# LayerNorm's transposed tiles copied whole by ScalarE and scaled in SBUF by GpSimd, four shared PSUM banks for TensorE's products, and one convolution chunk on TensorE in 5 bands of 15 instead of 7

## The chip, the cores and the metric

The kernel runs on one core of one Trainium2 chip. The metric is device time in microseconds (us); lower is better. The core has five engines with an instruction queue each, executed in order: TensorE (PE in the profile; PEld is its weight load), VectorE (DVE), ScalarE (ACT), GpSimd (POOL) and SyncE (SP, which here only issues DMAs). Engines wait for one another by semaphores. TensorE's results land in PSUM, of which this kernel uses eight banks; VectorE and ScalarE read PSUM and SBUF, GpSimd reads SBUF alone in this kernel.

## What is computed

One transformer block on images, float32, for `x` of shape (16, 128, 96, 96): 16 images, 128 channels, 96 by 96 pixels.

```python
def _ffn(xn_nchw, w_in, w_dw, w_out):
    h1 = jnp.einsum('bchw,oc->bohw', xn_nchw, w_in[:, :, 0, 0])           # 128 -> 512 channels
    h2 = lax.conv_general_dilated(h1, w_dw, ..., feature_group_count=HID) # 3x3, each channel by itself
    h3 = jax.nn.gelu(h2, approximate=False)
    return jnp.einsum('bchw,oc->bohw', h3, w_out[:, :, 0, 0])             # 512 -> 128
...
xn1 = _layernorm(x_hwc, ln1_w, ln1_b)              # over the 128 channels of a pixel
attn_out = _attention(xn1, wq, wk, wv, wp)         # channel attention: 8 heads of 16 x 16
x = x + attn_out.transpose(0, 3, 1, 2)
xn2 = _layernorm(x_hwc, ln2_w, ln2_b).transpose(0, 3, 1, 2)
x = x + _ffn(xn2, w_in, w_dw, w_out)
```

`_layernorm` subtracts the mean over the channels and divides by the square root of the variance plus 1e-5.

## The kernel before

**Tiling.** Channels lie on the 128 partitions, pixels along the free dimension. An image has 8 bands of 12 rows (1152 pixels); 16 images give 128 bands. A band has three units of 4 rows (384 pixels) and 9 blocks of 128 pixels. A quad is four such blocks (`QT = 4`, 512 pixels); an image has 18 quads, and each goes through LayerNorm twice (`norm`, with `second` false and true; the profile's names end in `_a` and `_b`), so there are 576 quads in all.

**LayerNorm of one quad** (functions `pixels` and `channels` inside `norm`). `forth` (L642) has TensorE transpose the four 128 x 128 blocks into one PSUM bank `tr`, pixels then on the partitions. `stats` (L649) has VectorE take mean and variance, two blocks per `bn_stats` instruction, directly out of that bank. GpSimd adds the epsilon (`variance`, L656), takes the power -0.5 (`power`, L660) and, in the second norm, computes minus the mean (L664) and the shift (L668). `scaled` (L700, L704) has ScalarE read each block from the bank and write it, scaled, to an SBUF tile `zT`: four instructions of 128 x 128. Only then is the bank free for the next quad. For the first norm `gram` (L714) multiplies the scaled blocks with themselves for the attention. `back` (L753) transposes three blocks (a unit) back into a bank `h`, and `place` (L757, L759) has ScalarE copy them to the padded image tile `xn`. For image 0 the transposes go to the accumulator's banks, and VectorE scales two of the four blocks (`also_scaled`, L687 and L691).

**Attention and second sum.** `attention` is a short chain of small steps per image. `x2` then multiplies a unit of `xn` with the image's 128 x 128 matrix (`mix`, L595); ScalarE writes the result (`mixed`, L604), and a GpSimd-issued DMA adds `x` to it in place (`add_x`, L607).

**Feed-forward.** The 512 hidden channels are four chunks of 128. A chunk of a band is one job (`conv_job`): three matmuls for the hidden values (`hidden`, L940) into banks `h`, ScalarE copies them to a padded tile (`kept`, L945; `halo`, L936), and the nine taps of the 3 x 3 filter are shared out. ScalarE multiplies three taps (`products`, L956). GpSimd adds one of them to the centre tap (`merge`, L959), and issues two accumulating DMAs that add the others to one another and to the result (L978, L981). VectorE runs five taps: the first from SBUF with the merged tile into the PSUM accumulator `acc` (L965), three that add into `acc` (L969), and the last from `acc` to the SBUF tile `h3` (L965 too). ScalarE applies gelu (L985). In the first chunk of every eighth band, 16 jobs in all, GpSimd and not ScalarE multiplies the third tap (`POOL_THIRDS`, L954).

In some bands, chosen by `by_pe`, the fourth chunk (`PE_CHUNK`) has no such job: TensorE runs its nine taps as matmuls with `w_in` folded into the weights (`by_matmuls`, L1043: 9 taps x 3 units = 27 matmuls), and ScalarE only applies gelu out of the bank (L1053). Counting from the end of the kernel, the last eight bands have their own list (`PE_LAST`, 5 of 8), and of each further 15 bands those with a number in `PE_BANDS` are done so: 7 of 15. That makes 61 bands of 128 with a TensorE chunk and 451 jobs.

At the end of a band, `ffn_out` multiplies the four `h3` tiles with `w_out` (L1070, four matmuls a unit), VectorE adds the result to the residual (L1077), and SyncE stores the band (L1081).

A float32 matmul shows as two TensorE instructions in the trace, so 27 matmuls are 54 rows; a transpose is one.

**PSUM.** Eight banks: three for the accumulator `acc`, one for the attention `g`, one for the LayerNorm transposes (`TR_BANKS = 1`) and three (`H_BANKS`) for everything else TensorE puts out: `hidden`, `back`, `mix`, the TensorE convolution and `ffn_out`.

**What sets the order.** Each engine's queue is written out before the kernel runs by a planner (class `Plan`). Every piece of work is an operation with an engine, a guessed duration, its reads and writes, and a place: its position in the kernel plus an offset of its kind from the table `AT`. `Plan.order` lets a clock run over guessed durations; whenever an engine is idle it takes the ready operation with the lowest place, if its buffers are free. Pools in `IN_TURN` hand out buffers strictly by place. The chip then runs these queues in the planned order with semaphore waits, however long things really take.

```python
def pool(ns, p, f, r, w):
    op("POOL", ns, p, f, r, w, ns + 80 + SLACK, ns + 80)
...
if o[9]:
    rest = max(0, self.held - time)
```

The last lines are the planner's account of VectorE's operations marked `two` (the first tap, with two SBUF inputs): it lets these and GpSimd's operations wait for one another.

Of the kernel before, what the change touches and what calls it, by code (L numbers as in the profile page):

```python
# [20 lines left out]
PE_BANDS = (0, 2, 4, 6, 8, 10, 12)  # L21
# [10 lines left out]
POOL_THIRDS = ((0, 8, (0,)),)  # L32
# [3 lines left out]
H_BANKS = 3  # L36
TR_BANKS = 1
# [3 lines left out]
XB_BUFS = 6  # L41
PR_BUFS = 6
H3_BUFS = 8
ZT_BUFS = 3
IN_TURN = ("tr", "h3", "pr", "xb", "x1")
AT = dict(
    load_w=-23.15, weights=8.85, zeros=-516.75, load_a=-160.1, forth_a=-16.1, stats_a=-17.05, variance_a=183.35,
    power_a=301.95, pool_product=152.05, merge=156.45, scaled_a=-1137.4, gram=-0.85, back_a=-14.1, place_a=-95.4,
    attention=-155.65, mix=-11.85, residual=204, mixed=-1141.25, add_x=299.05, forth_b=-13.55, stats_b=-99.2,
    variance_b=21.65, power_b=-40.55, shift_b=20.9, scaled_b=-2169.3, back_b=-9.7, place_b=-55.15, halo=-1095.75,  # L50
    hidden=1.05, kept=-147.7, products=153.4, add_last=168, tap=2.3, add_first=200.7, gelu=-155.2, conv=2.15,
    conv_gelu=1.35, out=4.45, add=-621.65, store=-160.45, mix_0=-13.8, residual_0=-1573.7, mixed_0=-58.5,
    add_x_0=27.15, gram_0=-2.5, forth_a_0=-17.8, forth_b_0=-14.9, stats_a_0=-680.6, stats_b_0=-1576.65,
    scaled_a_0=-21.75, scaled_b_0=-1153.5, back_a_0=51.9, back_b_0=-16.75, place_a_0=250.55, place_b_0=-28.05,
    shift_b_0=22.8, late=-1575.85,
# [10 lines left out]
T_MERGE = 2600  # L66
T_POOL_PRODUCT = 1750
# [3 lines left out]
class Plan:  # L71
# [7 lines left out]
    def __init__(self, **pools):  # L79
        self.free = {p: list(range(n)) for p, n in pools.items()}  # L80
        self.slot = {}
        self.ops, self.writer, self.readers, self.users = [], {}, {}, {}
        self.dma = 0.0
        self.two = self.held = self.lost = 0.0
# [31 lines left out]
    def order(self):  # L116
# [38 lines left out]
        def dispatch(engine, time):  # L155
# [73 lines left out]
def tile_restormer_block(  # L229
# [180 lines left out]
    def dve(ns, p, f, r, w, two=False):  # L410
        op("DVE", ns, p, f, r, w, ns + 120 + SLACK, ns, two=two)

    def pool(ns, p, f, r, w):
        op("POOL", ns, p, f, r, w, ns + 80 + SLACK, ns + 80)
# [164 lines left out]
    def norm(i, second, place_of):  # L579
# [41 lines left out]
        def pixels(s, m):  # L621
# [6 lines left out]
            def tr_of(q):  # L628
                return ("acc", q % ACC_BANKS) if early else (key_, (name, q))
# [3 lines left out]
            def forth(q):  # L633
                if early:
                    of = acc_banks[:, q % ACC_BANKS * 4 * P : (q % ACC_BANKS + 1) * 4 * P]
                else:
                    of = bank((name, q)) if key_ == "h" else trs_[plan.slot["tr", (name, q)]]
# [6 lines left out]
            def stats(j):  # L644

                if j == 0:
                    d["st"] = small.tile([P, QB * QT // 2, 6], F32, tag="st", name=f"st_{name}_{m}")
                h, k = divmod(2 * j, QT)
                nc.vector.bn_stats(  # L649
                    d["st"][:, j, :], d["pT", qs[h]][:, k : k + 2, :].rearrange("p t c -> p c t")  # L650
                )
# [9 lines left out]

            def minus():
                d["nm"] = small.tile([P, QB * QT], F32, tag="nm", name=f"nm_{name}_{m}")
                nc.gpsimd.tensor_scalar(d["nm"], d["mv"][:, :, 1], -1.0, 0.0, ALU.mult, ALU.add)  # L664

            def shift():
                nb = d["nb"] = small.tile([P, QB * QT], F32, tag="nb", name=f"nb_{name}_{m}")
                nc.gpsimd.tensor_tensor(nb, d["nm"], d["rstd"], ALU.mult)  # L668
# [14 lines left out]
            def also_scaled(q):  # L683
                for k in range(by_dve):
                    t = (q - qs[0]) * QT + k
                    if not second:
                        nc.vector.tensor_scalar(  # L687
                            zT(q)[:, k, :P], d["pT", q][:, k, :], d["rstd"][:, t : t + 1], None, ALU.mult
                        )
                        continue  # L690
                    nc.vector.tensor_scalar(  # L691
                        zT(q)[:, k, :P], d["pT", q][:, k, :], d["mv"][:, t, 1:2], d["rstd"][:, t : t + 1],
                        ALU.subtract, ALU.mult,
                    )

            def scaled(q):
                for k in range(by_dve, QT):
                    t = (q - qs[0]) * QT + k
                    if not second:
                        nc.scalar.activation(  # L700
                            zT(q)[:, k, :P], d["pT", q][:, k, :], AF.Copy, scale=d["rstd"][:, t : t + 1]
                        )
                        continue
                    nc.scalar.activation(  # L704
                        zT(q)[:, k, :P], d["pT", q][:, k, :], AF.Identity,
                        bias=d["nb"][:, t : t + 1], scale=d["rstd"][:, t : t + 1],
                    )
# [12 lines left out]
            for q, tr in zip(qs, trs):  # L720
                units = {t // TPU: None for t in range(q * QT, (q + 1) * QT)}
                pe(112 * QT, at("forth" + ab, s, i), lambda q=q: forth(q), [xtok(u) for u in units], [tr])
            for j in range(QB * QT // 2):
                dve(341, at("stats" + ab, s, i), lambda j=j: stats(j), [trs[2 * j // QT]], [bt])
            pool(T_SMALL, at("variance" + ab, s), variance, [], [bt])
            if second:
                pool(T_SMALL, at("variance" + ab, s), minus, [], [bt])
            pool(T_POWER, at("power" + ab, s), power, [], [bt])
            if second:
# [425 lines left out]
```

## Time and profile before

| | us |
|---|---|
| median of three runs | 4684.66 (4675.91 to 4693.29) |
| the profiled execution, its own time | 4687.34 |
| its span in the trace | 4685.6 |
| granted TensorE clock | 0.984 |

The profiled execution lies 2.7 us above the median; its span leaves out 1.7 us at the ends.

How to read the lines that follow. In part 1 of the page, each engine has its busy time, the share of the span and its instruction count. Part 4 follows the work that ended last back to the start: at each instruction to whatever released it. The shares say how much of the span each engine and line filled on that chain. A group of instructions reads: line, engine, operation, output<-input, sizes, count | total busy time in us, mean duration of one in ns | idle time of the engine just before them, and what ended it. Total busy time over count is less than the mean duration where instructions overlap on their engine. A row of waits reads: engine and line, the line that released it, total us, how many times, the longest. The answer for one line gives durations as minimum/median/maximum in ns. A table of stretches gives, for a stretch of the span, the busy time of each engine with its instruction count.

### The profile page before, as it was taken

Reading aid. Unit: us, or ns where it says so; the run is one execution under the profiler, and the core shown is the slowest. Engines: PE = TensorE matmul, PEld = TensorE weight load, DVE = VectorE, ACT = ScalarE, POOL = GpSimd, SP = SyncE. Lnnn points to the kernel's source line nnn. Section 1 sums busy time; section 2 is a strip of 40 time slices with the busy share of each in tenths; the row PEclk is TensorE's granted clock in tenths of the full one; section 3 lists DMA queues with packets and bytes.
Section 4 is the critical chain, followed back from the end, with each engine's and each line's share of the span. In section 5 each row is a group of like instructions: output and inputs, shape, how many; then the busy total and the mean of one; then the engine's idle time right before and its main releaser. Section 6 shows DMA issues by size and latency. Waiting matters only on the chain.

```text
span 4685.6 us, 53625 instructions
## 1 busy us (share of the span) xinstructions
PE 4250.4 (91%) x17217; PEld 2638.8 (56%) x17217; DVE 3766.1 (80%) x4096; ACT 4052.6 (86%) x7299; POOL 2950.8 (63%) x3271
## 2 busy tenths in 40 slices
PE   7999899888998989989899898999999999999899
PEld 5555555555555655545555555555555555555455
DVE  5988787877878778787778886888878877887878
ACT  4998888988989888898888888889989888998986
POOL 4666666666756666666666665766666666665653
PEclk9999999999999999999999999999999999999999
DMA  2878687777878768777778886887878878787786
GB/s 73 177 162 171 147 182 162 162 160 154 175 163 168 165 144 176 164 159 163 160 162 167 169 177 135 179 170 163 182 148 177 171 157 169 158 182 154 156 162 147
DMA packets 186955, 758.12 MB, mean 162 GB/s; under 512 B 21680, under 2 KB 23088, under 8 KB 186672
## 3 DMA queue, kind: packets, MB, share of 16 engines
q0 software_dynamic: 147168, 602.87, 68.3%
q1 hardware_dynamic: 38256, 151.73, 9.0%
q8 instruction: 136, 2.23, 0.2%
q14 instruction: 147, 1.20, 0.1%
q10 hardware_dynamic: 1248, 0.09, 0.0%
HBM read 148.26 MB, written 75.50 MB: 48 GB/s over the span
## 4 chain that ended last, share of the span: by engine, by line
PE 36%; DVE 26%; ACT 20%; issue 7%; DMA 7%; POOL 4%; DVEq 0%; POOLq 0%; ACTq 0%
DVE acc L969 13%; PE h L1070 10%; PE h L1043 10%; ACT pr L956 7%; PE h L940 6%; DMA h<-pr 5%; DVE acc L965 5%; DVE h L965 4%; ACT h L945 3%; ACT zT L704 2%; PE h L753 2%; PE tr L642 2%; ACT h L985 2%; PE g L714 2%; ACT zT L700 2%
## 5 line engine op out<-in xcount | busy, mean ns | idle before, releaser
L969 DVE SCALAR_TENSOR_TENSOR acc<-h,ratio,acc 128x1140 f32<-128x1140 f32 (+2 forms) x1356 | 1873.9, 1382 | 32.9
L956 ACT ACTIVATE pr<-h,ratio 128x1152 f32<-128x1152 f32 x1334 | 1695.7, 1309 | 46.0 <-DMA pr<-pr 22.6
L959 POOL TENSOR_TENSOR merged<-pr,h 128x1152 f32<-128x1152 f32 x450 | 1142.3, 2539 | 220.7 <-ACT pr L956 171.5
L1070 PE MATMUL h<-h,woutT 128*128 128x384 f32 x3072 | 1143.1, 498 | 52.8 <-ACT h L945 21.5
L1043 PE MATMUL h<-xn,comp 128*128 128x380 f32 (+1 forms) x3294 | 1148.6, 483 | 16.5 <-DVE x L1077 7.9
L940 PE MATMUL h<-xn,winT 128*128 128x384 f32 (+2 forms) x2706 | 1064.8, 504 | 89.5 <-DVE x L1077 30.4
L1043 PEld LDWEIGHTS h<-xn,comp 128*128 128x128 f32 x3294 | 607.1, 189 | 405.8 <-DVE x L1077 13.8
L1070 PEld LDWEIGHTS h<-h,woutT 128*128 128x128 f32 x3072 | 570.1, 193 | 453.3 <-ACT h L945 43.4
L965 DVE SCALAR_TENSOR_TENSOR acc<-h,ratio,merged 128x1152 f32<-128x1152 f32 x450 | 640.5, 1423 | 193.9 <-POOL merged L959 164.2
L945 ACT COPY h<-h 128x384 f32<-128x384 f32 (+2 forms) x1353 | 657.2, 523 | 138.9 <-PE h L940 122.2
L940 PEld LDWEIGHTS h<-xn,winT 128*128 128x128 f32 x2706 | 483.1, 191 | 476.9 <-ACT h L945 77.5
L981 POOL DMA_DIRECT2D h<-pr x450 | 432.4, 961 | 452.6 <-DVE h L965 95.2
L965 DVE SCALAR_TENSOR_TENSOR h<-h,ratio,acc 128x1152 f32<-128x1152 f32 x451 | 636.2, 1411 | 38.4 <-PE h L1070 26.8
L985 ACT ACTIVATE h<-h 128x1152 f32<-128x1152 f32 x453 | 539.0, 1190 | 77.7 <-DMA h<-pr 71.1
L978 POOL DMA_DIRECT2D pr<-pr x450 | 420.7, 937 | 224.4 <-ACT pr L956 187.8
L704 ACT ACTIVATE zT<-tr,nb_b,rstd_b 128x128 f32<-128x128 f32 x1132 | 432.1, 485 | 66.2 <-POOL nb_b L668 64.9
L642 PE MATMUL tr<-ident,x 128*128 128x128 f32 x2212 | 347.4, 280 | 122.6 <-ACT zT L704 63.4
L642 PEld LDWEIGHTS tr<-ident,x 128*128 128x128 f32 x2212 | 262.2, 142 | 340.9 <-ACT zT L700 129.2
L753 PE MATMUL h<-ident,zT 128*128 128x128 f32 x2304 | 373.9, 282 | 62.7 <-ACT h L945 38.6
L649 DVE BATCH_NORM_STATS2 st_b<-tr 128x6 f32<-128x256 f32 x566 | 214.6, 421 | 215.5 <-PE tr L642 214.6
L649 DVE BATCH_NORM_STATS2 st_a<-tr 128x6 f32<-128x256 f32 x540 | 205.1, 421 | 217.9 <-PE tr L642 217.5
L700 ACT ACTIVATE zT<-tr,rstd_a 128x128 f32<-128x128 f32 x1080 | 314.2, 396 | 47.2 <-POOL rstd_a L660 43.0
(172 smaller groups left out, 3968.9 us busy)
## 6 DMA issues: line engine op xcount, KB each, us to landing
pr<-pr POOLq DMA_DIRECT2D x450, 576.0 KB, 5.6
h<-pr POOLq DMA_DIRECT2D x450, 576.0 KB, 6.5
x<-in_x_dram SPq DMA_DIRECT2D x128, 576.0 KB, 5.6
out_dram<-x SPq DMA_DIRECT2D x127, 576.0 KB, 5.1
x<-in_x_dram POOLq DMA_DIRECT2D x122, 576.0 KB, 6.3
out_dram<-x SPq DMA_DIRECT2D x3, 192.0 KB, 1.9
weights<-in_L_conv_w_in_dram SPq DMA_DIRECT2D x1, 256.0 KB, 3.0
weights<-in_L_conv_w_out_dram SPq DMA_DIRECT2D x1, 256.0 KB, 3.2
```

The costliest lines, as they stand in the source:

```text
L642: nc.tensor.transpose(d["pT", q][:, k, :], xt[:, j * P : (j + 1) * P], ident)
L704: nc.scalar.activation(zT(q)[:, k, :P], d["pT", q][:, k, :], AF.Identity, bias=d["nb"][:, t : t + 1], scale=d["rstd"][:, t : t + 1],)
L753: nc.tensor.transpose(d["pB"][:, j * P : (j + 1) * P], zTs[q][:, k, :P], ident)
L940: nc.tensor.matmul(rows(ph), lhsT=winT[:, n, :], rhs=window(xn, r0 + r, e - r, 1), start=True, stop=True)
L945: nc.scalar.copy(window(h1_, r, e - r, 1), rows(d.pop(("ph", r))))
L956: nc.scalar.activation(to, shifted(t), AF.Copy, scale=ratio[:, n, t : t + 1])
L959: nc.gpsimd.tensor_tensor(merged, d["pr", dma_taps[0]], shifted(UNIT), ALU.add)
L965: nc.vector.scalar_tensor_tensor(to, shifted(t), ratio[:, n, t : t + 1], also, ALU.mult, ALU.add)
L969: nc.vector.scalar_tensor_tensor(to, shifted(t)[:, lo:hi, cut], ratio[:, n, t : t + 1], to, ALU.mult, ALU.add)
L985: nc.scalar.activation(h3, h3, AF.Gelu)
L1043: nc.tensor.matmul(d["pc"][:, lo:hi, cut], lhsT=comp[:, t, :], rhs=window(xn, r0 + dy, UR, dx)[:, lo:hi, cut], start=(t == order[0]), stop ...
L1070: nc.tensor.matmul(rows(d["po"]), lhsT=woutT[:, n, :], rhs=h3s[g, n][:, s * UR : (s + 1) * UR, :], start=(k == 0), stop=(k == NCH - 1),)
```

## The change

Three things change, and the planner's table of offsets with them.

1. **LayerNorm.** `forth` transposes as before. ScalarE then copies the whole 128 x 512 bank into the SBUF tile `zT` in one instruction (`copied`), which frees the bank. `stats` reads the `zT` tile, with its blocks 129 elements apart. GpSimd scales each block in place, one instruction of 128 x 128 each (`scaled`); for the second norm that instruction subtracts the mean and multiplies, so minus-the-mean and the shift are gone. For image 0 VectorE scales two of the four blocks in SBUF. There are five `zT` tiles instead of three, one buffer less for residual bands (`XB_BUFS` 6 to 5), and `zT` tiles are handed out in turn.
2. **PSUM.** The separate `tr` bank joins the others: four banks shared by all of TensorE's products and transposes. Three TensorE operations are now planned only once what they lead to is free: `hidden` when its rows of the padded tile are, `back` when its unit of `xn` is, and the first `ffn_out` matmul of a unit when all four `h3` tiles are ready.
3. **Convolution.** `PE_BANDS` has 5 entries of 15 instead of 7. With the last eight bands as before, 45 bands have a TensorE chunk and 467 jobs run the other way. `POOL_THIRDS` is empty, so ScalarE does every third tap.

The planner's durations change for the merge, GpSimd's product and the scaling, VectorE's operations get 120 ns for a follower on their own engine, and its account of `two` counts GpSimd's pieces singly.

```diff
-PE_BANDS = (0, 2, 4, 6, 8, 10, 12)
+PE_BANDS = (0, 3, 6, 9, 12)
...
-POOL_THIRDS = ((0, 8, (0,)),)
+POOL_THIRDS = ()
...
-H_BANKS = 3
-TR_BANKS = 1
+H_BANKS = 4
+TR_BANKS = 0
...
-XB_BUFS = 6
+XB_BUFS = 5
...
-ZT_BUFS = 3
-IN_TURN = ("tr", "h3", "pr", "xb", "x1")
+ZT_BUFS = 5
+IN_TURN = ("zT", "tr", "h3", "pr", "xb", "x1")
 AT = dict(
...
-T_MERGE = 2600
-T_POOL_PRODUCT = 1750
+T_MERGE = 2430
+T_POOL_PRODUCT = 1190
+T_SCALED = 240
...
-                self.held = time + ns
-            if o[9]:
-                rest = max(0, self.held - time)
+                self.held, self.piece = time + ns, ns / (o[9] or 1)
+            if o[9] and engine == "DVE":
+                rest = min(self.piece, max(0, self.held - time))
...
-                    d["st"][:, j, :], d["pT", qs[h]][:, k : k + 2, :].rearrange("p t c -> p c t")
+                nc.vector.bn_stats(d["st"][:, j, :], zT(qs[h])[:, k : k + 2, :P].rearrange("p t c -> p c t"))
...
+            def copied(q):
+                nc.scalar.copy(zT(q)[:, :, :P], d["pT", q])
+
+            def scaled(engine, q, ks):
+                for k in ks:
                     t = (q - qs[0]) * QT + k
+                    z, rstd = zT(q)[:, k, :P], d["rstd"][:, t : t + 1]
+                    if second:
+                        engine.tensor_scalar(z, z, d["mv"][:, t, 1:2], rstd, ALU.subtract, ALU.mult)
+                    else:
+                        engine.tensor_scalar(z, z, rstd, 1.0, ALU.mult, ALU.mult)
...
-                act((QT - by_dve) * (343 if second else 250), at("scaled" + ab, sh, i), lambda q=q: scaled(q), [tr, bt], [(*zt, 1)])
+                pool((QT - by_dve) * T_SCALED, at("scaled" + ab, sh, i), lambda q=q: scaled(nc.gpsimd, q, range(by_dve, QT)), [bt], [(*zt, 1)] if by_dve else [(*zt, 0), (*zt, 1)], QT - by_dve)
...
-            pe(t_mm((e - r) * W), at("hidden", jk), lambda r=r, e=e: hidden(r, e), [*zs, ("w", "in")], [ph])
+            pe(t_mm((e - r) * W), at("hidden", jk), lambda r=r, e=e: hidden(r, e), [*zs, ("w", "in")], [ph, *to])
```

More of the change, by code (lines that the diff above doesn't have):

```diff
@@ L40 @@
 X1_BUFS = 2
-XB_BUFS = 6
+XB_BUFS = 5
 PR_BUFS = 6
 H3_BUFS = 8
-ZT_BUFS = 3
-IN_TURN = ("tr", "h3", "pr", "xb", "x1")
+ZT_BUFS = 5
+IN_TURN = ("zT", "tr", "h3", "pr", "xb", "x1")
 AT = dict(
[L47 to L55, printed above, removed]
+    load_w=-88.85, weights=84.15, zeros=-584.25, load_a=-90.25, forth_a=0.1, stats_a=210.8, variance_a=469.5,
+    power_a=-191.15, pool_product=152.05, merge=-624.25, scaled_a=-827.6, gram=1176.3, back_a=6.5, place_a=-978.8,
+    attention=-91.2, mix=271.55, residual=204, mixed=-120.4, add_x=-2320.5, forth_b=3.85, stats_b=-9.7,
+    variance_b=-113.9, power_b=-208.85, shift_b=20.9, scaled_b=-200.85, back_b=274.95, place_b=-72.05, halo=-401.1,
+    hidden=349.8, kept=296.55, products=533.05, add_last=-206.35, tap=-16.6, add_first=-3299.75, gelu=408.9,
+    conv=2403.85, conv_gelu=-18.6, out=961.7, add=-6, store=-101.05, mix_0=-8.05, residual_0=75.4, mixed_0=15.8,
+    add_x_0=-1947.05, gram_0=-3.95, forth_a_0=-6.3, forth_b_0=-2.4, stats_a_0=-3302.15, stats_b_0=308.15,
+    scaled_a_0=-625.1, copied_a=-218.3, copied_b=-73.2, copied_a_0=531.1, copied_b_0=-227.2, scaled_b_0=-3302.4,
+    back_a_0=6.5, back_b_0=269.9, place_a_0=-234.3, place_b_0=531.1, shift_b_0=22.8, late=-54.8,
 )
@@ L410, in dve, with pool @@
     def dve(ns, p, f, r, w, two=False):
-        op("DVE", ns, p, f, r, w, ns + 120 + SLACK, ns, two=two)
-    def pool(ns, p, f, r, w):
-        op("POOL", ns, p, f, r, w, ns + 80 + SLACK, ns + 80)
+        op("DVE", ns, p, f, r, w, ns + 120 + SLACK, ns + 120, two=two)
+    def pool(ns, p, f, r, w, pieces=1):
+        op("POOL", ns, p, f, r, w, ns + 80 + SLACK, ns + 80, two=pieces)
     def add(p, f, r, w):
```

62 lines of the change are left out of this document (15 added, 47 removed).

## The prediction

> **What bounds the kernel now.** I read the page's busy times first, then its chain of waits.
>
> ```profile
> span 4685.6 us, 53625 instructions
> PE 4250.4 (91%) x17217; PEld 2638.8 (56%) x17217; DVE 3766.1 (80%) x4096; ACT 4052.6 (86%) x7299; POOL 2950.8 (63%) x3271
> PE 36%; DVE 26%; ACT 20%; issue 7%; DMA 7%; POOL 4%; DVEq 0%; POOLq 0%; ACTq 0%
> DVE acc L969 13%; PE h L1070 10%; PE h L1043 10%; ACT pr L956 7%; PE h L940 6%; DMA h<-pr 5%; DVE acc L965 5%; DVE h L965 4%; ACT h L945 3%; ACT zT L704 2%; PE h L753 2%; PE tr L642 2%; ACT h L985 2%; PE g L714 2%; ACT zT L700 2%
> ```
>
> TensorE is busiest, but holds only 36% of the chain: the bound changes hands. Two stretches next to one another show it:
>
> ```profile
> 2605.00:2617.00 12.00, 10.22 (x38) 5.55 (x38) 2.55 (x5) 11.94 (x26) 7.39 (x10) 1.00 0.89 162
> 2640.00:2675.00 35.00, 31.43 (x131) 20.07 (x130) 34.09 (x33) 31.21 (x55) 24.23 (x26) 0.99 0.91 190
> ```
>
> The columns are the stretch, its length, then busy PE, PEld, DVE, ACT, POOL. In the first VectorE works 2.55 of 12 us while ScalarE and TensorE are full; in the second, taps without a TensorE chunk, VectorE works 34.09 of 35. So work taken off one engine pays only for the part of it that lies on the chain. I use, for each group, chain time over busy time as the price of a microsecond moved. Who waits for whom:
>
> ```profile
> PE tr L642 <- ACT zT L704: 63.4, 58, 6.4
> PE tr L642 <- ACT zT L700: 56.3, 61, 2.2
> DVE st_a L649 <- PE tr L642: 217.5, 92, 6.5
> DVE st_b L649 <- PE tr L642: 214.6, 77, 7.4
> DVE acc L965 <- POOL merged L959: 164.2, 64, 6.1
> ```
>
> Transposes wait 120 us for the one `tr` bank that ScalarE's scaling still holds, and VectorE stands 432 us before statistics that come late from TensorE. VectorE's first tap waits 164 us for GpSimd's merge: GpSimd is 63% busy and already late at places.
>
> **Part A: sixteen convolution chunks leave TensorE.** 61 bands minus 45 is 16 bands: 432 matmuls of L1043 go (864 rows, two a matmul), 48 hidden matmuls (96 rows) come, and 16 jobs come for the other engines.
>
> ```profile
> L1043 PE MATMUL h<-xn,comp 128*128 128x380 f32 (+1 forms) x3294 | 1148.6, 483 | 16.5 <-DVE x L1077 7.9
> L940 PE MATMUL h<-xn,winT 128*128 128x384 f32 (+2 forms) x2706 | 1064.8, 504 | 89.5 <-DVE x L1077 30.4
> L956 ACT ACTIVATE pr<-h,ratio 128x1152 f32<-128x1152 f32 x1334 | 1695.7, 1309 | 46.0 <-DMA pr<-pr 22.6
> L945 ACT COPY h<-h 128x384 f32<-128x384 f32 (+2 forms) x1353 | 657.2, 523 | 138.9 <-PE h L940 122.2
> L936 ACT COPY h<-h 128x192 f32<-128x192 f32 x343 | 137.0, 399 | 0.0
> L985 ACT ACTIVATE h<-h 128x1152 f32<-128x1152 f32 x450 | 537.6, 1195 | 72.2 <-DMA h<-pr 71.1
> L1053 ACT ACTIVATE h<-h 128x384 f32<-128x384 f32 x183 | 94.8, 518 | 51.7 <-PE h L1043 51.1
> L969 DVE SCALAR_TENSOR_TENSOR acc<-h,ratio,acc 128x1140 f32<-128x1140 f32 (+2 forms) x1356 | 1873.9, 1382 | 32.9
> L965 DVE SCALAR_TENSOR_TENSOR acc<-h,ratio,merged 128x1152 f32<-128x1152 f32 x450 | 640.5, 1423 | 193.9 <-POOL merged L959 164.2
> L965 DVE SCALAR_TENSOR_TENSOR h<-h,ratio,acc 128x1152 f32<-128x1152 f32 x451 | 636.2, 1411 | 38.4 <-PE h L1070 26.8
> L959 POOL TENSOR_TENSOR merged<-pr,h 128x1152 f32<-128x1152 f32 x450 | 1142.3, 2539 | 220.7 <-ACT pr L956 171.5
> L981 POOL DMA_DIRECT2D h<-pr x450 | 432.4, 961 | 452.6 <-DVE h L965 95.2
> ```
>
> - TensorE: 864 x 1148.6/3294 = -301 us; 96 x 1064.8/2706 = +38. L1043 holds 10% of 4685.6, 469 us of its 1148.6 on the chain: price 0.41, so -123. L940 holds 6%, 281 of 1064.8: 0.26, so +10.
> - VectorE: 16 x (1.423 + 3 x 1.382 + 1.411) = +112. Price 26% x 4685.6 / 3766.1 = 0.32: +36.
> - ScalarE: 64 products (48 of the new jobs, 16 from GpSimd) at 1695.7/1334 us, +81; 48 copies at 657.2/1353, +23; 28 halo copies more, +11; 16 gelus, +19; 48 small gelus fewer, -25: +110. Price 20% x 4685.6 / 4052.6 = 0.23: +25.
> - GpSimd: 16 merges and 32 DMA issues, 16 x 2.539 + 32 x 0.961 = +71, counted in Part B. The two accumulations of a job are 32 transfers more beside 1022 of GpSimd's (450 each of two kinds and 122 sums of `x`), 3% of a DMA load that is not full even in the stretch shown (0.91); I add nothing.
>
> Without GpSimd the move brings 52 us: little, since VectorE and ScalarE pay it back.
>
> **Part B: LayerNorm.**
>
> ```profile
> L704 ACT ACTIVATE zT<-tr,nb_b,rstd_b 128x128 f32<-128x128 f32 x1132 | 432.1, 485 | 66.2 <-POOL nb_b L668 64.9
> L700 ACT ACTIVATE zT<-tr,rstd_a 128x128 f32<-128x128 f32 x1080 | 314.2, 396 | 47.2 <-POOL rstd_a L660 43.0
> L945 ACT COPY h<-h 128x384 f32<-128x384 f32 x1024 | 499.0, 521 | 113.9 <-PE h L940 97.7 <-DVE h L965 10.3 <-DVE x L1077 2.3
> L945 ACT COPY h<-h 128x480 f32<-128x480 f32 x216 | 121.1, 582 | 14.3 <-PE h L940 14.1
> L649 DVE BATCH_NORM_STATS2 st_b<-tr 128x6 f32<-128x256 f32 x566 | 214.6, 421 | 215.5 <-PE tr L642 214.6
> L845 DVE TENSOR_TENSOR wide<-g,wqkT 128x256 f32<-128x256 f32 x15 | 6.3, 418 | 4.0 <-ACT wide L841 4.0
> L877 DVE TENSOR_SCALAR kq<-g,rn 128x128 f32<-128x128 f32 x15 | 5.1, 342 | 0.0
> L891 DVE TENSOR_TENSOR em<-e,blocks 128x128 f32<-128x128 f32 x16 | 4.5, 282 | 0.0
> L668 POOL TENSOR_TENSOR nb_b<-nm_b,rstd_b 128x4 f32<-128x4 f32 x288 | 116.0, 403 | 11.5
> L664 POOL TENSOR_SCALAR nm_b<-st_b 128x4 f32<-128x4 f32 x288 | 66.9, 232 | 22.6
> L656 POOL TENSOR_SCALAR ve_a<-st_a x288: 184/194/1421, 8.5 to 4292.8; 128x4 f32<-128x4 f32 x144
> L954 POOL TENSOR_SCALAR pr<-h,ratio 128x1152 f32<-128x1152 f32 x16 | 19.6, 1225 | 15.2 <-ACT h L945 14.6
> L660 POOL TENSOR_TENSOR rstd_b<-ve_b,mhalf x288: 997/1032/2346, 91.4 to 4565.1; 128x4 f32<-128x4 f32 x144
> ```
>
> - ScalarE loses L704 and L700, 746 us, and gets 576 copies of 128x512. Busy time of a copy is 0.487 us at 384 columns and 0.561 at 480, so 0.586 at 512: +337. Net -409. L704 and L700 hold 2% each, 187 us of 746: price 0.25, -102.
> - VectorE's 1152 statistics read SBUF. A 128x128 instruction from PSUM took 342 ns (L877), one from SBUF 282 (L891): 60 ns less, -69 us, price 0.32: -22. What the far-apart blocks cost there, no row shows; that is a rival.
> - GpSimd gets 2258 scalings of 128x128. 194 ns at 4 columns and 1225 at 1152 make 0.9 ns a column and 305 ns at 128: +689 us. Bounds: 194 (438 us in all) and, if a column cost what the merge's does (2539 ns over 1152, 2.2), 194 + 124 x 2.2 = 467 ns (1054 us). I take 305, since L954 is the same operation. Off go L664, L668 and L954: -203. With Part A's 71: +557. Its price lies between GpSimd's own now (4% x 4685.6 / 2950.8 = 0.06) and VectorE's 0.32, which GpSimd will come near with 3508 us, 75% of the span. I take 0.2, the middle: +111 (33 to 178; by the scaling's own bounds, at 0.2, 61 to 184).
> - The added waits: each scaling waits on GpSimd for statistics and power, and behind it in that queue stand merges and the issues of accumulations; for those wait VectorE's first taps (164 us now) and ScalarE's gelu. This is what the 0.2 pays for. In exchange a quad may stay longer under way: five `zT` tiles instead of three.
>
> **Part C: the banks.** The three `h` banks are filled 3072 times (1353 hidden, 768 `back`, 384 `mix`, 384 `ffn_out`, 183 convolution); afterwards 3072 again plus 553 transposes on four, 906 a bank instead of 1024, and a transposed bank is freed by one copy, not after statistics, power and scaling. The 120 us of transposes waiting could go; but the copy takes its turn in ScalarE's queue. I take half, -60 (0 to -120). The later planning of `hidden`, `back` and `ffn_out` adds no instruction. One residual band fewer in flight I cost at nothing: five bands are 5/8 of an image, which covers the lead of the mix over the store; without that cover `mix` would join TensorE's waits.
>
> **Sum** against the profiled execution's 4687.3: -123 + 10 + 36 + 25 - 102 - 22 + 111 - 60 = -125, 4562; the shown median is 2.7 lower, so I forecast **4560 us**. With the low ends of GpSimd and banks: 4560 - 78 - 60 = 4422; with the high ends 4560 + 67 + 60 = 4687.
>
> **Rivals.**
>
> 1. *TensorE stays the bound and keeps its share.* Its work becomes 4250.4 - 301 + 38 = 3987; at today's 4250.4/4685.6 = 0.907 that is 4395. For it: 91% has been held with two others at 80 and 86%. Against: afterwards VectorE has 3809, ScalarE 3754 and GpSimd 3508, all within 12% of TensorE.
>
> 2. *GpSimd becomes the bound: slower.* A first tap of VectorE with two SBUF inputs stops GpSimd:
>
> ```profile
> 2617.47 1.43 DVE L965 SCALAR_TENSOR_TENSOR acc<-h,ratio,merged 128x1152 f32<-128x1152 f32 x1 [3.32 <-POOL merged L959]
> 2617.52 1.42 POOL L664 TENSOR_SCALAR nm_b<-st_b 128x4 f32<-128x4 f32 x1
> L959 POOL TENSOR_TENSOR merged<-pr,h x450: 2411/2430/3421, 113.4 to 4653.4; 128x1152 f32<-128x1152 f32 x150
> L965 DVE SCALAR_TENSOR_TENSOR acc<-h,ratio,merged x450: 1404/1425/1433, 116.9 to 4659.3; 128x1152 f32<-128x1152 f32 x150
> ```
>
> L664, 194 ns elsewhere, lasted 1.42 us under the tap. So GpSimd's need is its undisturbed work, 466 x 2.43 + 1055 issues x 0.96 + 576 x (0.194 + 1.032) + 689 = 3540, plus up to 466 x 1.425 = 664 of taps: 4204, 90% of 4685. At ScalarE's present share of 0.865 that gives 4860; at TensorE's 0.907, 4635. It decides for slower once GpSimd cannot be kept over 90% in its fixed order; I call it **4780**, between. For it: GpSimd stands idle 221 us before merges and 453 us before L981 now, at the head of an ordered queue. Against: not every tap finds GpSimd with work.
>
> [...]
>
> 3. *Statistics out of SBUF cost more.* `bn_stats` takes two blocks in turn, 129 elements apart. In PSUM the jump is free: 421 ns beside 418 for a plain 256 columns (L845). If each element cost two accesses in SBUF, an instruction would cost some 256 x 1.2 ns (L969's 1382 ns over 1140) = 307 ns more: 354 us busy instead of -69, at 0.32 +135, so **4695**. No row is for or against. [...]
>
> 4. *The change does not free what it says*: the bank waits for the copy as it waited for scaling, and ScalarE's saved time lies beside other work. Without Part C's 60 and the 102: **4722**.
>
> **How the numbers follow.** Forecast (4470 to 4660) 0.45, rival 1 0.17, rival 2 0.18, rival 3 0.10, rival 4 0.10. About 0.5%, 23 us, can be told from no change: faster is below 4661, slower above 4708. Faster: 0.43 + 0.17 + 0.02 + 0.03 + 0.02 = 0.67; same: 0.02 + 0.03 + 0.03 + 0.03 = 0.11; slower: rival 2 0.13, rival 3 0.04, rival 4 0.05 = 0.22. The range reaches to rivals 1, 3 and 4 and towards rival 2: **4390 to 4770**; the forecast's own is 4420 to 4690.
>
> **What would show it.** Right: TensorE's busy time near 3990; no transpose waiting over 60 us in all; ScalarE near 3750; a scaling near 305 ns and GpSimd's busy time near 3510 plus more stops under taps; statistics near 360 ns; GpSimd's share of the chain near 10%. Wrong: statistics over 450 ns (rival 3); first taps waiting 400 us for the merge and GpSimd over 85% busy (rival 2); TensorE still at 90% (rival 1); transposes waiting for copies (rival 4).

## The result, and the profile after

| | before | changed |
|---|---|---|
| median, us | 4686.3 (4 runs, 4675.9 to 4693.3) | 4745.5 (4 runs, 4741.6 to 4752.4) |
| ratio to before, 95% interval | | 1.013 (1.0107 to 1.0152) |
| span of the profiled execution, us | 4685.6 | 4739.9 |
| granted TensorE clock | 0.984 | 0.965 |

The change made the kernel 1.3% slower, where a gain to 4560 us had been forecast. Part 1 of the changed kernel's page, then the groups that answer to the prediction's rows:

```profile
PE 4170.1 (88%) x16449; PEld 2569.5 (54%) x16449; DVE 3849.8 (81%) x4173; ACT 3769.9 (80%) x5728; POOL 4301.0 (91%) x4988
L682 POOL TENSOR_SCALAR zT<-zT,st_b,rstd_b 128x128 f32<-128x128 f32 x1142 | 1096.3, 1139 | 5.8
L684 POOL TENSOR_SCALAR zT<-zT,rstd_a 128x128 f32<-128x128 f32 x1116 | 457.3, 453 | 23.8
L935 POOL TENSOR_TENSOR merged<-pr,h 128x1152 f32<-128x1152 f32 x466 | 1248.3, 2679 | 52.5 <-ACT pr L932 23.5
L729 PE MATMUL h<-ident,zT 128*128 128x128 f32 x2304 | 530.9, 298 | 415.2 <-POOL zT L682 320.7
L643 PE MATMUL h<-ident,x 128*128 128x128 f32 x2212 | 333.0, 284 | 38.9 <-DMA x<-in_x_dram 21.6
L675 ACT COPY zT<-h 128x512 f32<-128x512 f32 x553 | 313.9, 595 | 116.3 <-PE h L643 112.1
```

GpSimd has gone from 63% to 91% and is now the busiest engine; TensorE, ScalarE and VectorE all have room. L682 and L684 are the new scalings, of the second and the first norm. They have the same shape and nearly the same count, yet L682 took 1096 us and L684 457. The transposes back to channels (L729) now stand idle 415 us, 392 of them before scaled tiles (320.7 for L682 and 71.3 for L684): the forward transposes' wait (L643, 123 us before, nearly all of it for the bank, and 39 now) shrank, and a longer one came one step later. The two lines by themselves, durations as minimum, median and maximum:

```profile
L682 POOL TENSOR_SCALAR zT<-zT,st_b,rstd_b x1142: 778/906/2978, 78.5 to 4657.6; 128x128 f32<-128x128 f32 x191
L684 POOL TENSOR_SCALAR zT<-zT,rstd_a x1116: 359/373/2135, 10.7 to 4327.9; 128x128 f32<-128x128 f32 x186
```

Even the shortest L682, 778 ns, is twice the median L684, 373. The difference in the code is small: L684 is z times rstd times 1.0, with one per-partition operand; L682 is z minus mean, times rstd, with two.

Two neighbouring stretches, to be held against the two of before (length, then busy PE, PEld, DVE, ACT, POOL):

```profile
3000.00:3040.00 40.00, 34.34 (x142) 21.57 (x140) 31.28 (x34) 33.34 (x49) 39.34 (x48) 0.97 0.86 183
3040.00:3080.00 40.00, 36.40 (x145) 22.18 (x145) 33.24 (x35) 31.30 (x49) 39.21 (x46) 1.00 0.82 167
```

The bound no longer changes hands: GpSimd works 39.3 of 40 us in one and 39.2 in the other, and no other engine is full in either.

A single statistics instruction, out of SBUF with its blocks 129 elements apart, takes as long as before:

```profile
L650 DVE BATCH_NORM_STATS2 st_b<-zT 128x6 f32<-128x256 f32 x576 | 244.2, 428 | 115.8 <-ACT zT L675 113.6 <-POOL zT L684 1.2
```

428 ns stands beside 421 out of PSUM. In busy time it became dearer: 244.2/576 = 0.424 us each against 214.6/566 = 0.379, since these instructions now hardly overlap with their neighbours; what ended the overlap, no run shows.

### The profile page after: what moved, and what is told of

Its sections match the earlier page's. It is cut to its first block, busy times and chain, and to the rows that moved or that the text cites. A ratio compares the mean times of both kernels' runs of the same rounds, so it can differ in the third digit from the quotient of the medians.

```text
span 4739.9 us, 52491 instructions
## 1 busy us (share of the span) xinstructions
PE 4170.1 (88%) x16449; PEld 2569.5 (54%) x16449; DVE 3849.8 (81%) x4173; ACT 3769.9 (80%) x5728; POOL 4301.0 (91%) x4988
## 5 line engine op out<-in xcount | busy, mean ns | idle before, releaser
L935 POOL TENSOR_TENSOR merged<-pr,h 128x1152 f32<-128x1152 f32 x466 | 1248.3, 2679 | 52.5 <-ACT pr L932 23.5
L682 POOL TENSOR_SCALAR zT<-zT,st_b,rstd_b 128x128 f32<-128x128 f32 x1142 | 1096.3, 1139 | 5.8
L1019 PE MATMUL h<-xn,comp 128*128 128x380 f32 (+2 forms) x2430 | 904.3, 493 | 2.7 <-ACT xn L733 1.8
L729 PE MATMUL h<-ident,zT 128*128 128x128 f32 x2304 | 530.9, 298 | 415.2 <-POOL zT L682 320.7
L941 DVE SCALAR_TENSOR_TENSOR acc<-h,ratio,merged 128x1152 f32<-128x1152 f32 x466 | 674.6, 1448 | 173.4 <-POOL merged L935 161.6
L729 PEld LDWEIGHTS h<-ident,zT 128*128 128x128 f32 x2304 | 307.0, 142 | 758.5 <-POOL zT L682 483.2
L1019 PEld LDWEIGHTS h<-xn,comp 128*128 128x128 f32 x2430 | 453.3, 196 | 266.0 <-issue 31.3
L954 POOL DMA_DIRECT2D pr<-pr x466 | 479.4, 1029 | 93.9 <-ACT pr L932 67.1
L1053 DVE TENSOR_TENSOR x<-h,x 128x384 f32<-128x384 f32 x384 | 212.9, 555 | 337.4 <-PE h L1046 311.3
L684 POOL TENSOR_SCALAR zT<-zT,rstd_a 128x128 f32<-128x128 f32 x1116 | 457.3, 453 | 23.8
L675 ACT COPY zT<-h 128x512 f32<-128x512 f32 x553 | 313.9, 595 | 116.3 <-PE h L643 112.1
L643 PE MATMUL h<-ident,x 128*128 128x128 f32 x2212 | 333.0, 284 | 38.9 <-DMA x<-in_x_dram 21.6
```

The lines of the kernel that those rows point to most:

```text
L682: engine.tensor_scalar(z, z, d["mv"][:, t, 1:2], rstd, ALU.subtract, ALU.mult)
L729: nc.tensor.transpose(d["pB"][:, j * P : (j + 1) * P], zTs[q][:, k, :P], ident)
L935: nc.gpsimd.tensor_tensor(merged, d["pr", dma_taps[0]], shifted(UNIT), ALU.add)
L941: nc.vector.scalar_tensor_tensor(to, shifted(t), ratio[:, n, t : t + 1], also, ALU.mult, ALU.add)
L954: nc.gpsimd.dma_start(out=d["pr", dma_taps[1]], in_=d["pr", t], accum_op=ALU.add)
L1019: nc.tensor.matmul(d["pc"][:, lo:hi, cut], lhsT=comp[:, t, :], rhs=window(xn, r0 + dy, UR, dx)[:, lo:hi, cut], start=(t == order[0]), stop ...
```

## The experiments

Twelve kernels ran, each timed against the kernel before on the same chip (three rounds, but for the one on instruction forms). The theory: the second norm's scaling instruction is slow on GpSimd and fills it. The rivals: the convolution's move, the lower clock, queues ordered for a wrong duration, and, inside the theory, two per-partition operands, the subtraction, or 'the lock with VectorE': that the scaling owes its 906 ns to VectorE's work beside it, as L664, 194 ns at the median, lasted 1.42 us under a first tap in the kernel before.

| run | us | ratio, 95% interval | PE / DVE / ACT / POOL busy, us | clock |
|---|---|---|---|---|
| changed kernel | 4745.5 | 1.013 (1.011 to 1.015) | 4170 / 3850 / 3770 / 4301 | 0.965 |
| e1 one operand | 4330.0 | 0.924 (0.923 to 0.925) | 4030 / 3817 / 3736 / 3811 | 0.983 |
| e2 changed, 7 bands | 4855.8 | 1.036 (1.035 to 1.038) | 4358 / 3742 / 3717 / 4203 | 0.972 |
| e3 before, 5 bands | 4862.3 | 1.038 (1.036 to 1.040) | 4182 / 3878 / 4121 / 3052 | 0.948 |
| e5 planner told | 4633.6 | 0.989 (0.987 to 0.991) | 4097 / 3859 / 3756 / 4286 | 0.947 |
| e6 add | 4436.3 | 0.947 (0.945 to 0.949) | 4069 / 3830 / 3747 / 3966 | 0.975 |
| e7 folded | 4324.0 | 0.923 (0.922 to 0.925) | 4023 / 3821 / 3736 / 3822 | 0.988 |
| e8 one operand, 7 bands | 4433.7 | 0.947 (0.945 to 0.948) | 4203 / 3725 / 3686 / 3700 | 0.993 |
| e9 add, planner told | 4395.6 | 0.939 (0.937 to 0.941) | 4020 / 3845 / 3732 / 3977 | 0.973 |
| e10 folded, planner told | 4287.7 | 0.915 (0.914 to 0.917) | 3992 / 3826 / 3723 / 3773 | 0.978 |
| e11 folded, wide | 4120.2 | 0.879 (0.878 to 0.881) | 3900 / 3867 / 3711 / 3440 | 0.987 |
| e12 centred, wide | 4180.6 | 0.892 (0.891 to 0.894) | 4004 / 3889 / 3718 / 3452 | 0.992 |

**e1: one operand in both norms.**

```diff
-                    if second:
-                        engine.tensor_scalar(z, z, d["mv"][:, t, 1:2], rstd, ALU.subtract, ALU.mult)
-                    else:
-                        engine.tensor_scalar(z, z, rstd, 1.0, ALU.mult, ALU.mult)
+                    engine.tensor_scalar(z, z, rstd, 1.0, ALU.mult, ALU.mult)
```

The second norm's mean is not subtracted at all here, so this kernel does not compute the block; it serves to price the instruction.

> The changed kernel, with the second norm's scaling done as the first norm's: one per-partition operand (z times rstd times 1.0) instead of two (z minus mean, times rstd). The mean's subtraction is left out of the second norm, nothing else; the order of every queue is the same. Theory 'two operands': the 1142 instructions of L682 took 906 ns at the median, L684's only 373, so GpSimd loses some 1142 x (0.96 - 0.41) = 630 us of its 4301 busy us, is no longer the bound, and the time falls to 4500 to 4620 us, under the kernel before. Rival 'the convolution': the sixteen jobs moved off TensorE are what costs; then the time stays above 4690. Rival 'the granted clock' (0.965 instead of 0.984): the time stays near 4740 whatever GpSimd does.

4330 us: 415 us less than the changed kernel and 7.6% less than before, beyond what was expected. Its part 1, the engines' line of its chain, and the scalings of both norms:

```profile
PE 4029.8 (93%) x16449; PEld 2528.6 (58%) x16449; DVE 3817.4 (88%) x4173; ACT 3736.3 (86%) x5728; POOL 3810.7 (88%) x4988
POOL 39%; PE 23%; DVE 13%; ACT 9%; issue 9%; DMA 8%; POOLq 0%; ACTq 0%; DVEq 0%
L681 POOL TENSOR_SCALAR zT<-zT,rstd_b 128x128 f32<-128x128 f32 x1142 | 539.9, 549 | 23.3
L681 POOL TENSOR_SCALAR zT<-zT,rstd_a 128x128 f32<-128x128 f32 x1116 | 474.4, 501 | 20.2
```

The same 1142 blocks cost GpSimd 540 us instead of 1096, and every queue is in the changed kernel's order. One operation in one instruction turns a loss of 1.3% into a gain of 7.6%; the convolution's move and the clock are not what cost the time. (The clock recovered with it, to 0.983. But e5 below is 112 us faster than the changed kernel at 0.947, so here the time does not follow the clock.)

**e4: the forms alone.** GpSimd runs 24 instructions of each form on a 128x128 tile, then 8 of some on 128x512, with VectorE idle.

```python
nc.gpsimd.tensor_scalar(z(k), z(k), r(k), 1.0, ALU.mult, ALU.mult)         # L38
nc.gpsimd.tensor_scalar(z(k), z(k), m(k), r(k), ALU.subtract, ALU.mult)    # L40
nc.gpsimd.tensor_scalar(z(k), z(k), r(k), m(k), ALU.mult, ALU.add)         # L42
nc.gpsimd.tensor_scalar(z(k), z(k), r(k), m(k), ALU.mult, ALU.mult)        # L44
nc.gpsimd.tensor_scalar(z(k), z(k), m(k), 1.0, ALU.subtract, ALU.mult)     # L46
nc.gpsimd.tensor_scalar(z(k), z(k), 0.25, 1.0, ALU.subtract, ALU.mult)     # L48
...                                                                        # 512 columns:
nc.gpsimd.tensor_scalar(big, big, rs[:, 0:1], 1.0, ALU.mult, ALU.mult)     # L50
nc.gpsimd.tensor_scalar(big, big, st[:, 0, 1:2], rs[:, 0:1], ALU.subtract, ALU.mult)   # L52
nc.gpsimd.tensor_tensor(big, big, rs.unsqueeze(2).to_broadcast([P, 4, P]), ALU.mult)   # L54
```

> No part of the block is computed here, x is copied to the output; GpSimd alone runs forms of the scaling on 128x128, 24 each, nothing else on VectorE. Theory 'two operands': one per-partition operand takes 340 to 380 ns, two take 800 to 900, whatever the operations (subtract and multiply, multiply and add, multiply twice), and the 512-column forms show the difference per column. Rival 'the subtraction': subtract with one per-partition operand is slow too and multiply-and-add with two is fast. Rival 'the lock with VectorE': all forms take about 310 ns here, and the 906 ns came from VectorE beside it.

Its groups on GpSimd, with the busy time and the mean duration of one in ns:

```profile
L40 POOL TENSOR_SCALAR z<-z,st,rs 128x128 f32<-128x128 f32 x24 | 18.6, 792 | 0.0
L46 POOL TENSOR_SCALAR z<-z,st 128x128 f32<-128x128 f32 x24 | 16.7, 717 | 0.0
L52 POOL TENSOR_SCALAR z<-z,st,rs 128x512 f32<-128x512 f32 x8 | 16.4, 2070 | 0.0
L48 POOL TENSOR_SCALAR z<-z 128x128 f32<-128x128 f32 x24 | 14.6, 642 | 0.0
L42 POOL TENSOR_SCALAR z<-z,rs,st 128x128 f32<-128x128 f32 x24 | 10.3, 449 | 0.0
L44 POOL TENSOR_SCALAR z<-z,rs,st 128x128 f32<-128x128 f32 x24 | 10.3, 448 | 0.0
L38 POOL TENSOR_SCALAR z<-z,rs 128x128 f32<-128x128 f32 x24 | 8.3, 372 | 0.1
L54 POOL TENSOR_TENSOR z<-z,rs 128x512 f32<-128x512 f32 x8 | 8.0, 1038 | 0.0
L50 POOL TENSOR_SCALAR z<-z,rs 128x512 f32<-128x512 f32 x8 | 5.4, 692 | 0.0
```

The rival won here: it is the subtraction. With no per-partition operand at all a subtraction takes 642 ns (L48), while multiply and add with two such operands takes 449 (L42) and one operand 372 (L38). One more per-partition operand added about 75 ns in each of three pairs of forms (372 to 448, L38 and L44; 642 to 717, L48 and L46; 717 to 792, L46 and L40). Per column, subtract and multiply costs (2070 - 792)/384 = 3.3 ns, multiply alone (692 - 372)/384 = 0.83. VectorE's work beside it is not the cause, since VectorE is idle here. In the changed kernel a scaling took 0.96 us of busy time (1096.3/1142) against 0.78 here (18.6/24), some 210 us more in all. The trace of the changed kernel ties most of that to VectorE's first taps: the 318 scalings of L682 that ran beside a first tap lasted 1657 ns on average, while the other 824 had a median of 797, close to the 792 alone.

**e6: an add in the subtraction's place.**

```diff
-                        engine.tensor_scalar(z, z, d["mv"][:, t, 1:2], rstd, ALU.subtract, ALU.mult)
+                        engine.tensor_scalar(z, z, d["nm"][:, t : t + 1], rstd, ALU.add, ALU.mult)
...
+            def minus():
+                d["nm"] = small.tile([P, QB * QT], F32, tag="nm", name=f"nm_{name}_{m}")
+                nc.gpsimd.tensor_scalar(d["nm"], d["mv"][:, :, 1], -1.0, 0.0, ALU.mult, ALU.add)
...
+            if second:
+                pool(T_SMALL, at("variance" + ab, s), minus, [], [bt])
```

> The changed kernel, whole, with the second norm's scaling as (z plus minus-the-mean) times rstd: an add in the subtraction's place, and the 288 small instructions that give minus the mean, as the kernel before had them. Alone, multiply and add with two per-partition operands took 449 ns against 792. Theory 'the instruction': 1142 x 0.34 = 390 us off GpSimd's 4301, 60 us of small instructions on: about 3970; from the one-operand run (3811 busy, 4330 us) and the changed kernel (4301, 4746), 4440 to 4500 us. Rival 'two operands': as slow as the changed kernel, 4700 or more.

4436 us, 5.3% under the kernel before and 4 us below the expected range: the same number of per-partition operands, no subtraction. Its scalings of the second norm stand beside the changed kernel's 1096.3 us:

```profile
L686 POOL TENSOR_SCALAR zT<-zT,nm_b,rstd_b 128x128 f32<-128x128 f32 x1142 | 679.9, 833 | 5.2
```

It settles that it is the operation and not the operands, in the kernel as alone.

**e7: the mean folded into weights.** The matrices of `hidden` and of TensorE's convolution are multiplied once, at the start, with identity minus 1/128, and the scaling is e1's. The diff shows its core.

```diff
+            def mm():
+                v[key] = bank(("weights", key))[:, :n]
+                nc.tensor.matmul(v[key], lhsT=v["centre"], rhs=of(), start=True, stop=True)
...
+        centring("c_in", lambda: winT.rearrange("p n c -> p (n c)"), "in")
...
+            centring(f"c_{t0}", lambda ts=ts: comp[:, ts[0] : ts[-1] + 1, :].rearrange("p t c -> p (t c)"), "conv")
```

> The changed kernel with the one-operand scaling in both norms, and the second mean's subtraction folded into the feed-forward's weights once at the start (the weights of the hidden matmuls and of TensorE's convolution, multiplied with identity minus 1/128); this computes the block as long as the second norm's shift, zero in these inputs, has no mean over the channels. Theory 'the instruction': the time of the one-operand run, 4330 us, plus about 5 for the start: 4320 to 4350. Rival (the one-operand run is fast for the data it makes): above 4450.

4324 us: e1's time again, now with the mean taken off, so e1 was not fast for what it left out.

**e5, e9, e10: what the planner believes.** The instructions stay; only the duration in the planner changes, and with it the order.

```diff
-                pool((QT - by_dve) * T_SCALED, at("scaled" + ab, sh, i), ...
+                pool((QT - by_dve) * (840 if second else 340), at("scaled" + ab, sh, i), ...
```

(e9 has 420 and 340 on e6; e10 has 340 on e7.)

> The changed kernel, with the planner told what a scaling takes: 840 ns in the second norm and 340 in the first, instead of 240. The instructions are the same, only their order may differ. Theory 'the instruction' (GpSimd's subtract-and-multiply at 792 ns alone, 906 in the kernel, fills GpSimd): GpSimd has the same 4301 us to do, so the time stays above 4680. Rival 'the wrong duration' (the loss comes from queues ordered for 240 ns): a fall to 4600 us or less.

> The kernel with the add, its planner told 420 ns for a scaling of the second norm and 340 of the first. Telling the planner the true 840 took 112 us off the changed kernel, where it was 600 ns out; here it is out by 180 and 100 ns. Theory 'both the instruction and the plan's duration': 4380 to 4430 us. Rival 'any new order is as good as another fitted one': within 10 us of 4436, or above.

> The folded kernel with the planner told 340 ns for both scalings. It was 100 ns out. Theory 'both': a small gain, 4290 to 4324 us. Rival 'any new order': 4324 or above, since the offsets were fitted to 240.

e5 fell by 112 us to 4634, 1.1% under the kernel before, with GpSimd as busy as in the changed kernel (4286 of 4640 us). That hits neither expectation, since the fall is real and short of the rival's: part of the loss was queues written for scalings of 240 ns, and correcting that alone brings the time under the kernel before. Two rows of waits from e5 and two from the changed kernel:

```profile
PEld h L729 <- POOL zT L682: 196.2, 194, 9.7
PE h L729 <- POOL zT L682: 132.6, 138, 9.0
```

```profile
PEld h L729 <- POOL zT L682: 483.2, 566, 3.4
PE h L729 <- POOL zT L682: 320.7, 456, 3.2
```

A planner that knows the scaling's length puts other TensorE work before the transposes that need it: 138 waits instead of 456. e9 gained 41 us and e10 36 us from smaller errors, and the same waits shrank there too (from 89 to 40 times between e6 and e9, from 149 to 49 between e7 and e10). The tables of offsets came with 240 ns; a duration nearer the truth helped all three times all the same. e10 ended 2 us below its expected range.

**e2, e3, e8: the convolution's bands.** One line each: `PE_BANDS` with seven entries in the changed kernel (e2) and in e1 (e8), with five in the kernel before (e3).

> The changed kernel with the convolution's seven bands of 15 put back, LayerNorm and banks as changed. Theory 'two operands': GpSimd has 16 merges and 32 issues less, about 75 us with their stops, of 4301, so the time falls a little, 4660 to 4730 us, and GpSimd stays at 90% busy. Rival 'the convolution': 4600 us or less.

> The kernel before with the convolution's five bands of 15 alone. My sum gave this part -52 us without GpSimd: 4620 to 4680 us. Rival 'the convolution': 4740 us or more. Theory 'two operands' says nothing of this run, except that the loss of 1.3% is not found here.

> The one-operand run with seven bands of 15 on TensorE. It asks what the convolution's move is worth once GpSimd is not the bound. My sum gave the move -52 us without GpSimd: so here 4360 to 4400 us. Rival 'the offsets are fitted to the five bands' (the kernel before with five bands lost 3.8%, the changed kernel with seven lost 2.3%): 4430 us or more.

e2 came out above both its expectations. e3 came out where the rival 'the convolution' stood, at 4740 or more; but that rival also had e2 fall to 4600 or less, and with seven bands put back the changed kernel became slower instead. e8 came out as its rival had it. Seven bands cost 110 us in the changed kernel, where GpSimd had less to do than with five (4203 against 4301), and 104 in e1; five bands cost 179 us in the kernel before, where a gain of 52 was expected. In e3 VectorE has 3878 us, 112 more, as counted, and ScalarE 4121; TensorE has 4182, only 68 less where 263 were counted, at a granted clock of 0.948. Transposes and statistics wait longer:

```profile
DVE st_b L649 <- PE tr L642: 345.9, 121, 7.6
PE tr L642 <- ACT zT L704: 165.3, 104, 5.4
```

215 and 63 us had stood there. Either pattern under the other's table of offsets loses 2 to 4%. One reading is that each table belongs to its pattern of bands. For e8 there is another: with seven bands TensorE is busy 4203 of 4433 us, 95%, so that it may simply have too much to do. No run tells the two apart; what the move alone is worth, each side with offsets of its own, was not tried and stays open.

**e11, e12: one wide instruction a quad.** e4 had shown 512 columns with a repeated second input in 1038 ns, against four times 372 for a quad in four pieces (four times 346 in busy time, 8.3/24). e11 is that on e7; e12 has, instead of e7's folding, the mean taken off where the blocks are transposed (and the planner told 228 ns instead of 112 for such a transpose).

```diff
+                if engine is nc.gpsimd:
+                    z, t = zT(q)[:, ks[0] : QT, :P], (q - qs[0]) * QT + ks[0]
+                    rstd = d["rstd"][:, t : t + len(ks)].unsqueeze(2).to_broadcast([P, len(ks), P])
+                    nc.gpsimd.tensor_tensor(z, z, rstd, ALU.mult)
+                    return
...
-                pool((QT - by_dve) * T_SCALED, ...
+                pool((QT - by_dve) * 260, ...
```

and in e12 besides

```diff
+    centre = const.tile([P, P], F32, name="centre")
+    nc.vector.tensor_scalar(centre, ident, -1.0 / C, None, ALU.add)
...
+                    if second:
+                        nc.tensor.matmul(d["pT", q][:, k, :], lhsT=xt[:, j * P : (j + 1) * P], rhs=centre, start=True, stop=True)
+                        continue
```

> The folded kernel with one 512-column multiply a quad in GpSimd, the four factors repeated along the columns as its second input, instead of four of 128; the planner is told 1040 ns a quad. Alone that instruction took 1038 ns, the four take some 1400 to 1490: about 576 x 0.4 = 230 us off GpSimd's 3822, to about 3590. Theory 'GpSimd still sets the end' (it holds 39% of the chain in the one-operand run): 4200 to 4290 us. Rival 'TensorE is the bound at 93%': 4310 or more.

> The changed kernel, whole and for any weights: the second norm's mean is taken off by TensorE, which multiplies each block with identity minus 1/128 where it transposed it; GpSimd scales a quad in one 512-column multiply, told at 1040 ns. Against the folded wide kernel (4120 us, TensorE 3900 busy) 1152 transposes of one row become float32 matmuls of two, about 0.14 us more each, 160 us of TensorE. Theory 'TensorE and VectorE are the bound now, at 95% and 94%': 4230 to 4300 us. Rival 'VectorE alone sets the pace': 4150 or less.

e11: 4120 us, 12.1% under the kernel before and 80 us under the expectation's lower end; GpSimd's busy time fell by 382 us from e7's, where 230 were expected. Against e10, whose planner also knows its scaling's duration, the wide instruction is worth 167 us. Its part 1 and the engines' line of its chain:

```profile
PE 3899.9 (95%) x16457; PEld 2500.9 (61%) x16457; DVE 3866.9 (94%) x4177; ACT 3711.1 (90%) x5728; POOL 3439.8 (83%) x3306
PE 30%; DVE 26%; ACT 15%; DMA 12%; POOL 9%; issue 7%; POOLq 0%; DVEq 0%; ACTq 0%
```

GpSimd, 39% of the chain in e1, holds 9%; TensorE and VectorE are at 95 and 94%. e12 pays for the centring on TensorE, 104 us of busy time and 60 of time rather than the 110 to 180 expected (its 1132 centring products in the trace took 296.3/1132 = 0.262 us of busy time each, a transpose in e11 322.0/2212 = 0.146: 0.12 us more where 0.14 was estimated), and needs no condition on the second norm's shift: 4181 us, 10.8% under the kernel before. Both beat both kernels.

## Why the prediction was wrong

**The step that failed** is in Part B: "I take 305, since L954 is the same operation." It is, for the first norm: z times a per-partition factor, 373 ns at the median against 305. The second norm's instruction subtracts, and that took 906 ns. I had put both into one term of 689 us; measured are 457.3 + 1096.3 = 1554. The upper bound of 1054 was no bound: it took the merge's time per column as the worst GpSimd does, at 2.2 ns, and subtract and multiply costs 3.3 alone (e4). The trace before held no subtraction on GpSimd and gave no warning.

**What followed from it.** GpSimd was forecast at 3508 us and measured 4301. That is rival 2, "GpSimd becomes the bound": 4780 was named and 4745.5 came, with GpSimd 91% busy, but with the scaling and not the stops under taps as the main price. It had a chance of 0.18; the forecast of a clear gain was on the wrong side. That 4745.5 lies inside the stated range of 4390 to 4770 is owed to the room given to that rival, not to the sum.

**A term that was missing.** The sum put nothing for what the planner believes. The change tells it 240 ns a scaling, while the sum itself used 305 and the chip took 373 and 906 at the median. Told 340 and 840, the same instructions ran 112 us faster (e5).

**The price of 0.2 per microsecond of GpSimd** failed with it. From e1 to the changed kernel GpSimd has 490 us more, and the time rises 415: 0.85. A price read from a chain is a price for that chain: GpSimd held 4% of the one this was read from, and holds 39% of e1's. Here, once GpSimd was 88 to 91% busy, its work cost close to its full amount. With the scalings at their measured 1554 us, the price of 0.2 would have given 4560 + 0.2 x 865 = 4733 us, near the measured time, but by luck: the price was four times too low, and the gain of all the rest was too low as well.

**With the scaling cheap, the rest of the sum was too small.** e1 gains 354 us (4683.6 to 4330.0) where my sum had -125, though its scalings still took 540 + 474 = 1014 us against the 689 of the sum. Rival 1, TensorE at an unchanged share, gave 4395 and was nearer. My reading is that chain prices of 0.2 to 0.4 undervalue work taken off engines that take turns as the bound; that is not shown, since no run here separates which of the changes to ScalarE, bank and bands brings how much of the 354.

**The other points.**
- The first of the two stretches was misread: TensorE is busy 10.22 of 12 us there, 85%, and only ScalarE, at 11.94, is full.
- Part A: the 52 us that the convolution's move was to bring did not show in e3, which lost 179 us; the sum priced the work and not the order of the queues, and what the move is worth under offsets of its own stays open.
- TensorE: 3987 forecast. 4170 came; most of the difference is in the transposes back, which wait for scaled tiles (L729 531 us where L753 had 374). In e10, where they wait little, TensorE has 3992. The work was counted rightly.
- ScalarE: 3754 forecast, 3770 measured. The copy was put at 0.586 us of busy time; 313.9/553 = 0.568. Right.
- VectorE: 3809 forecast, 3850 measured. Its statistics did not get 60 ns shorter out of SBUF: 487 us busy (244.2 and 242.7) instead of some 370. Rival 3, that an instruction would last some 307 ns longer, did not happen either: 428 ns against 421. Its two accesses an element in SBUF were my assumption; no run shows them.
- Banks (Part C): transposes waited 39 us where the sum left them 60, and 123 before. The wait moved to the transposes back, for GpSimd.
- Rival 4, that the bank waits for the copy, did not happen: of the 39 us that L643's matmuls waited, 3.2 were for ScalarE's copy (L675).
- First taps waited 162 us for the merge, as before (164), not the 400 named as the sign of rival 2: it was the scalings that came late, as the waits of L729 show.

## What to carry to other kernels

Before work is moved to an engine, look whether the trace holds that very operation there, operation by operation; if not, measure it alone first (here 24 instructions of each form told more than the whole profile). Where one operation is dear, look for another way to write it: here an add of the negative (e6, 5.3% under the kernel before), a fold into a weight (e7, 7.7%), and one wide instruction for four on top of the fold (e11, 12.1%). A planner that orders queues needs true durations; telling it a number nearer the truth gained 36 to 112 us without touching an instruction.

## What the runs showed of the hardware

- On GpSimd a subtraction in `tensor_scalar` took 642 ns at 128 columns where multiply and add with two per-partition operands took 449; per column 3.3 ns (subtract and multiply) against 0.83 (multiply), all measured in e4.
- VectorE's and GpSimd's instructions lasted longer beside one another, and both ways. In the kernel before only GpSimd's were seen to (L664 up to 1423 ns, 194 at the median; no first tap over 1433 ns, no product of L891 over 287). In the changed kernel a first tap lasted up to 1973 ns, and the attention's 128x128 product of two SBUF inputs averaged 807 ns instead of 282, by four long ones among 16 (2115 to 2504 ns; the median stayed at 284). One of the four, and the merge beside it (start and length in us):

```profile
L941 DVE SCALAR_TENSOR_TENSOR acc<-h,ratio,merged x466: 1397/1425/1973, 97.6 to 4706.9; 128x1152 f32<-128x1152 f32 x156
L867 DVE TENSOR_TENSOR em<-e,blocks 128x128 f32<-128x128 f32 x16 | 12.9, 807 | 0.0
2299.04 3.74 POOL L935 TENSOR_TENSOR merged<-pr,h 128x1152 f32<-128x1152 f32 x1
2300.44 2.50 DVE L867 TENSOR_TENSOR em<-e,blocks 128x128 f32<-128x128 f32 x1
```

  Each of the four long products began while a merge was under way and ended 0.16 us after it. The taps' median did not move (1425), so it cost them some 12 us in all (466 x (1448 - 1423) ns).
- `bn_stats`, which takes two blocks in turn, did not last longer with its blocks 129 elements apart in SBUF: 428 ns, against 421 out of PSUM. Whether a cheaper read from SBUF (in the kernel before a 128x128 instruction took 282 ns from there, L891, and one from PSUM 342, L877) and a dearer jump cancel there was not tried.
- Four engines were kept at 95, 94, 90 and 83% at once by an order planned before the run (e11); 91% for the busiest, as in both kernels, was no ceiling.
